# Three transfers of a fused kernel's opening are issued elsewhere: a bias on GpSimd's queue, second-layer weights behind turned blocks, and one tile's power between gathers

## The chip, the cores and the metric

The kernel runs on one core of a Trainium2 chip. Times are device microseconds of that core for one execution. The kernel before took 461.27 us in the median of three runs (460.65 to 464.81). Times in the profile are counted from the start of its span.

## The reference

The input `x` has 32 batches of 128 tokens with 512 features, all float32. Each batch has one row of conditioning `t`, and a mask that marks tokens. The reference is one block with two halves:

```
emb = silu(t) @ ada_w + ada_b;  shift, scale, gate = split(emb, 3)
norm = where(m, layernorm(x) * (1 + scale) + shift, 0)
fwd = gelu(norm @ ssm_w1 + ssm_b1) @ ssm_w2 + ssm_b2
bwd = flip(gelu(flip(norm) @ bwd_w1 + bwd_b1) @ bwd_w2 + bwd_b2)
x = x + gate * where(m, fwd + bwd, 0)
ff = silu(t) @ ffada_w + ffada_b;  shift2, scale2, gate2 = split(ff, 3)
h = gelu_tanh((layernorm(x) * (1 + scale2) + shift2) @ ff_w1 + ff_b1)
return x + gate2 * (h @ ff_w2 + ff_b2)
```

The first half counts only for the tokens that the mask marks, and these are the last tokens of each batch, at most 32 of them. The two flips cancel, since the layers work on each token alone. The second half is done for all 4096 tokens and holds most of the work.

## The kernel before

**Slots.** The marked tokens are gathered into 512 "slots", four tiles of 128. The first half is computed for slots only (`xc` holds their rows of `x`), and the new rows are written to memory in HBM, from which the second half gathers them over the rows of `x` that it has loaded. There are two such memories. `x1_wide` has the first two tiles of slots with mean and variance of each row beside it; `x1_rows` has all four tiles without them. If there are more slots, a loop at the end does the rest; in the profiled execution it does not run.

**Pairs.** The second half runs over four pairs of sides. A side is four batches, 512 tokens. Both of its matrix products are done by a Strassen-like scheme with seven products in place of eight. This needs sums of blocks of tokens (`TokenBlocks`, `token_sums`), and sums of blocks of weights: `fw1_of.combine` and `fw2_of.combine` change the weights in place, and `weight_sums(1)` to `weight_sums(4)` make further sums of the first layer's weights, which are stored to `t_rows` and loaded again for each pair (`load_weights`, into `tw`).

**Order.** The whole program is under a manual schedule: each engine works its instructions in the order in which they are written. The change lies in the opening, before the first pair's products:

- SP issues the loads of the weights and of `x`. Late among them are `raw[2]` and `raw[3]` (batches 4 to 7), the conditioning bias of the second half `modb_f` (L645, three loads of 64 KB, by `load_conditioning_bias`, L133) and its weights `ada_f` (L646, four loads of 768 KB). `modb_f` lies in the buffer of `modb_a`, the bias of the first half.
- `finish_slots(0, ...)` (L782) multiplies tile 0's result with its gate, adds `xc`, makes the statistics (`own_statistics`; its last step, the power -0.5, is on GpSimd, L178) and stores to `x1_wide` (L368) and `x1_rows` (L369).
- GpSimd gathers the new rows of batches 0 to 7 (`take_first_rows`, L792): batches 0 to 3 from tile 0 alone, 4 to 7 from tiles 0 and 1. Behind each of the first four gathers a memset on GpSimd releases one quarter of `fw2`'s load (`load_behind_gathers`, L139 and L136, 512 KB each). `finish_slots(1, ...)` stands after the third of them.
- VectorE normalises batches 0 to 3 (side 0, `normalised_of_side_0`) and transposes them in 32x32 blocks. Between the first two it makes `mod2` (`modulation_rows`, L313), the modulation of the second half, which TensorE transposes (`ptr_mod`, L850).
- TensorE goes on with the first half of slot tiles 2 and 3 (`hidden` and `project`, L207 and L224). In `hidden`, the table `after` puts other work behind each of its eight steps: `normalised_of_side_1` (batches 4 to 7), `turn_rows(0)` to `turn_rows(3)` (16 transfers of 64 KB that put side 0's blocks in place, shared by SP and ACT, L940), the stores of weight sums 1, 2 and 4, and after step 7 the two first combines of `fw2` on GpSimd and the loads for the second pair.
- `project` for tile 2 ("s2") is interleaved with TensorE's transposes of side 1 (`turn`, L929). `finish_late(2)`, `TokenBlocks.one(1)` to `one(4)` (L970) and `finish_late(3)` on VectorE follow, and TensorE starts the first pair's products (L1101), whose stream 5 is the first to read `tw`.

The transfers that SP and ACT issue share eight completion semaphores in turn: in the compiled program each of them waits for the one issued eight before it.

Of the kernel before, what the change touches and what calls it, by code (L numbers as in the profile page):

```python
# [9 lines left out]
F32 = mybir.dt.float32  # L10
# [12 lines left out]
def kernel(  # L23
# [49 lines left out]
    nc = tc.nc  # L73
    B, S, D = x.shape
    P = 128
    assert S == P
    G = 4
# [13 lines left out]
    stp = ctx.enter_context(tc.tile_pool(name="stp", bufs=4))  # L91
# [32 lines left out]
    def load_ada(t, w, blocks, width):  # L124

        for k in blocks:
            nc.sync.dma_start(t[:, k, :width], w[ts(k, P), :width])

    def load_conditioning_bias(t, vec, kinds, queue):

        rows = vec.rearrange("(m j c) -> m j c", m=3, c=P)
        for m in kinds:
            queue.dma_start(t[:, m], rows[m].unsqueeze(1).to_broadcast([KC, B, P]))  # L133

    def load_blocks(t, w):
        nc.sync.dma_start(t, w.rearrange("(k p) f -> p k f", p=P))  # L136

    def load_behind_gathers(t, w):
        nc.gpsimd.memset(t[0:1, 0, 0:1], 0.0)  # L139
        load_blocks(t, w)  # L140
# [7 lines left out]
    w2 = ssm.tile([P, HC, D], F32, name="w2")  # L148
# [20 lines left out]
    def own_statistics(t, n, name):  # L169

        for i in range(n):
            st = stp.tile([P, 6], F32, tag="st", name=f"st_{name}_{i}")
            row = t[:, i]
            nc.vector.bn_stats(st, row[:, :D])
            nc.vector.bn_aggr(row[:, D : D + 2], st)
        var = t[:, :, D + 1]
        nc.vector.tensor_scalar(var, var, EPS, None, ALU.add)
        nc.gpsimd.tensor_tensor(var, var, half[:, :n], ALU.pow)  # L178
# [22 lines left out]
    def hidden(xT, n, w, bcol, func, name, pool, parts=range(HC), after=None):  # L201

        h = []
        for f in parts:
            ph = ps_h.tile([P, 512], F32, tag="h", name=f"ph_{name}_{f}")
            for k in range(KC):
                nc.tensor.matmul(  # L207
                    ph[:, :n], w[:, k, ts(f, P)], xT[:, k, :], start=(k == 0), stop=(k == KC - 1)
                )
            t = pool.tile([P, n], F32, tag="h", name=f"h_{name}_{f}", bufs=HC)  # L210
            nc.scalar.activation(t, ph[:, :n], func, bias=biasT[:, bcol + f : bcol + f + 1])
            h.append(t)
            for g in (after or {}).get(f, ()):
                g()
        return h

    def project(i, h, w, name, between=None, bank=(ps_o, "o"), seeded=None):

        pool, tag = bank
        po = seeded or pool.tile([P, 512], F32, tag=tag, name=f"po_{name}_{i}")  # L220
        for f in range(HC):
            if between and f in between:
                between[f]()
            nc.tensor.matmul(  # L224
                po,
                h[f][:, ts(i, P)],
                w[:, f, :],
                start=(f == 0 and seeded is None),
                stop=(f == HC - 1),
                skip_group_check=seeded is not None,  # L230
            )
        return po

    def seeded_with_bias(at):
        po = ps_o.tile([P, 512], F32, tag="o", name=f"po_s{at}")
        nc.scalar.copy(po, b2)
        return po
# [111 lines left out]
    def gates_of_slots(tiles):  # L349

        strips = of_slots(
            pick, tiles, mod1, slice(2, 3), 2 * [(ps_o, "o")] + 2 * [(ps_t, "tr")], f"gate_s{tiles[0]}"
        )
        t = ssm.tile([P, len(tiles), D], F32, tag="gs", name=f"gs_{tiles[0]}")

        def to_sbuf():
            for j in range(KC):
                nc.scalar.copy(t[:, :, ts(j, P)], strips[j][:, :, 0])

        return [t[:, n] for n in range(len(tiles))], to_sbuf  # L360

    def finish_slots(at, po, gate):
        t = tp.tile([P, 1, D + 2], F32, tag="t", name=f"t_s_{at}")
        row = t[:, 0, :D]
        nc.vector.tensor_tensor(row, po, gate, ALU.mult)
        nc.vector.tensor_tensor(row, row, xc[at], ALU.add)
        own_statistics(t, 1, f"s_{at}_x1")
        nc.sync.dma_start(x1_wide[ts(at, P), :], t[:, 0])  # L368
        nc.sync.dma_start(x1_rows[ts(at, P), :], row)  # L369

    class Weights:

# [53 lines left out]
    x1_rows = dram.tile([NS, D], F32, name="x1_rows")  # L426
# [208 lines left out]
    fw2 = fwp.tile([P, HC, D], F32, name="fw2")  # L635
# [6 lines left out]
    load_raw(3)  # L642
    ada_f = adap.tile([P, KC, 3 * D], F32, tag="ada", name="ada_f")
    modb_f = adap.tile([P, 3, P], F32, tag="modb", name="modb_f", bufs=1)
    load_conditioning_bias(modb_f, ffada_b, range(3), nc.sync)  # L645
    load_ada(ada_f, ffada_w, range(KC), 3 * D)  # L646
    ph_s = {}

# [44 lines left out]
    def in_blocks(t):  # L693
        return t.rearrange("p g (h f) -> p (g h) f", f=2 * P)

    t_sum = {
        1: [in_blocks(t) for t in spare],
        2: [t_2[:, 0], t_2[:, 2]],
    }
# [17 lines left out]
    def store_weight_sums(*which, queue=nc.sync):  # L717
        for j in which:
            queue.dma_start(t_rows[j - 1, :, 4:], t_sum[j][1][:, :3])
            queue.dma_start(t_rows[j - 1, :, :4], t_sum[j][0])  # L720
# [30 lines left out]
    h1 = []  # L751
# [22 lines left out]
    gs, gates_to_sbuf = gates_of_slots(range(NC))  # L774
    po_s = [seeded_with_bias(0)]
# [3 lines left out]
    fw1_of.combine(0, 1, 2, 3)  # L779
    own_statistics(raw[2], 2, "x_2")  # L780
    b2_row = dram.tile([1, D], F32, name="b2_row")
    finish_slots(0, project(0, h1, w2, "s0", seeded=po_s[0]), gs[0])  # L782
    own_statistics(raw[3], 2, "x_3")
    t = in_blocks(group_of_tiles("tw_3"))
    t_sum[3] = [t[:, :4], t[:, 4:]]
# [4 lines left out]
    def take_first_rows(i):  # L790
        slots = P if i < G else NH
        nc.gpsimd.indirect_dma_start(  # L792
            out=raw[i // 2][:, i % 2],
            out_offset=None,
            in_=x1_wide[:slots],
            in_offset=bass.IndirectOffsetOnAxis(ap=slot_i[:, i : i + 1], axis=0),
            bounds_check=slots - 1,
            oob_is_err=False,
        )

    def take_first_rows_and_weights(i):
        take_first_rows(i)
        load_behind_gathers(fw2[:, ts(i, 2)], ff_w2[ts(i, 2 * P)])

    for i in range(3):
        take_first_rows_and_weights(i)
    finish_slots(1, project(1, h1, w2, "s1", seeded=po_s[1]), gs[1])
    take_first_rows_and_weights(3)
    for i in range(G, 2 * G):
        take_first_rows(i)  # L810

    for c in range(2):
# [43 lines left out]
    of_x = {}  # L856
# [6 lines left out]
    fw2_of = Weights(fw2, HC // 2, D // 2, t_2)  # L863
# [69 lines left out]
    def turned(xn, xT, queues, which=range(4)):  # L933

        R = 32
        src = xn.rearrange("p k i (q c) -> p q k i c", c=R)
        dst = xT.rearrange("p k (i b c) -> p b k i c", b=P // R, c=R)
        for b in which:
            for q in range(P // R):
                queues[(b + q // 2) % len(queues)].dma_start(dst[ts(q, R), b], src[ts(b, R), q])  # L940
# [406 lines left out]
    def turn_rows(b):  # L1347
        return lambda: turned(xn, xT[0], (nc.sync, nc.scalar), (b,))

    def combine_behind_weight_sums():  # L1350
        done = stp.tile([1, 1], F32, tag="done", name="done", bufs=1)
        nc.gpsimd.tensor_copy(done, t_sum[4][1][0:1, 2, 0:1])
        fw2_of.combine(0, 1, engine=nc.gpsimd)

    def load_of_pair_1():
        nc.sync.dma_start(b2_row, b2[0:1, :])
        broadcast_rows(fb2, ff_b2, nc.sync)
        x_of[1] = [load_side(1, 0, spare), None]
# [4 lines left out]
        3: [turn_rows(0), lambda: weight_sums(4)],  # L1363
        4: [turn_rows(1)],
        5: [turn_rows(2)],
        6: [turn_rows(3), lambda: store_weight_sums(1, 2, 4)],
        7: [combine_behind_weight_sums, load_of_pair_1],
    }
    h1 = hidden(xT_t, NH, w1, 0, AF.Gelu, "s1", ssm, after=after)
    nc.scalar.activation(warm, biasT[0:1, 0:1], AF.Gelu_apprx_tanh)  # L1370
# [12 lines left out]
    finish_late(2, project(0, h1, w2, "s2", {2 * k: turn(k) for k in range(KC)}, seeded=po_s[2]))  # L1383
    po = project(1, h1, w2, "s3", bank=(ps_h, "h"))
    of_x[0] = TokenBlocks(0, xT)
    for j in (1, 2, 3, 4):
        of_x[0].one(j)
    finish_late(3, po, b2)
    first_half.close()
# [285 lines left out]
```

## Time and profile before

| | us |
|---|---|
| median of the runs (lowest, highest) | 461.27 (460.65, 464.81) |
| the profiled execution | 461.85 |
| its span | 460.1 |
| busy in the span: TensorE | 448.6 |
| VectorE | 330.9 |
| ScalarE | 177.2 |
| GpSimd | 164.0 |
| mean granted TensorE clock | 0.995 |

The span is that of the profiled execution; 1.75 us of its time lie around it. An engine's busy time leaves out instructions that only issue transfers or wait. `PE` is TensorE's matmuls, `PEld` its weight loads, `DVE` VectorE, `ACT` ScalarE, `POOL` GpSimd, and `SP` the engine that mainly issues transfers; `SPq` and `ACTq` are their queues of instructions. `L368` is line 368 of the kernel. Names are the program's, with the buffer numbers left out, so `x_wide` is `x1_wide`, `fw` can be `fw1` or `fw2`, and `out<-in` says what an instruction writes and reads. A releaser (`<-DVE xn`) is what ended a wait, as the trace's semaphore events let one infer.

### The profile page before, as it was taken

What the parts mean: (1) busy time and instruction counts of PE and PEld (TensorE: products, weight loads), DVE (VectorE), ACT (ScalarE), POOL (GpSimd) and SP (SyncE); (2) the same over time, 40 slices, a digit from 0 to 9 for tenths busy, and PEclk for the clock granted to TensorE, in tenths of its full rate; (3) what the DMA queues carried; (4) which work ended last, traced back from release to release, by engine and by line L of the source; (5) the groups of instructions that cost most, each with busy time, mean ns of one, the idle gap of its engine ahead of it and who ended that gap; (6) DMA issues with size and microseconds to landing.
All of it is one profiled execution on the core that took longest, in us unless ns stands there. A gap on an engine that the chain in (4) does not pass through costs nothing.

```text
span 460.1 us, 6203 instructions
## 1 busy us (share of the span) xinstructions
PE 448.6 (97%) x2161; PEld 370.8 (81%) x2161; DVE 330.9 (72%) x568; ACT 177.2 (39%) x387; POOL 164.0 (36%) x158
## 2 busy tenths in 40 slices
PE   8999898999999999999999999999999999999995
PEld 3784485587888888888888888888888888888884
DVE  4798677879779849896786498967973996434645
ACT  3123114354355371344454614454446144552000
POOL 4210436058971000489700005887000026560000
PEclk9999989999999999999999999999999999999999
DMA  7999769772306743923087348220773342222022
GB/s 231 384 395 331 286 203 212 263 277 58 127 0 215 103 96 120 354 75 115 3 228 105 80 150 333 97 84 11 220 110 74 127 171 81 80 89 95 0 86 102
DMA packets 83405, 70.98 MB, mean 154 GB/s; under 512 B 63160, under 2 KB 64520, under 8 KB 82346
## 3 DMA queue, kind: packets, MB, share of 16 engines
q1 hardware_dynamic: 68438, 58.60, 40.9%
q0 software_dynamic: 4160, 10.54, 6.7%
q10 hardware_dynamic: 10772, 1.39, 2.2%
q8 instruction: 19, 0.31, 0.3%
q14 instruction: 16, 0.13, 0.1%
HBM read 56.84 MB, written 13.70 MB: 153 GB/s over the span
## 4 chain that ended last, share of the span: by engine, by line
PE 85%; DMA 6%; POOL 4%; issue 3%; DVE 2%; POOLq 0%; SPq 0%; DVEq 0%
PE a_o L1288 23%; PE a_m L1101 18%; PE e_o L1288 18%; PE e_m L1101 14%; PE po_s L224 5%; DMA x_wide<-t_s 3%; POOL x L869 2%; PE ph_s L656 2%; PE ph_s L207 2%; DMA xc<-in_x_dram,token_i_s 1%; POOL x L792 1%; DMA tw<-t_rows 1%; DMA x<-x_wide,slot_i 1%; PE last L1288 1%; PE pm_keep_clock L446 1%
## 5 line engine op out<-in xcount | busy, mean ns | idle before, releaser
L1152 POOL TENSOR_TENSOR ha<-p_m,ha 128x512 f32<-128x512 f32 x20 | 25.8, 1288 | 166.9 <-ACT ha L1159 142.1
L1288 PE MATMUL e_o<-fw,ha 128*128 128x256 f32 x256 | 57.9, 379 | 0.0
L923 ACT ACTIVATE xT<-xT,modT 128x128 f32<-128x128 f32 x112 | 44.2, 480 | 32.2 <-DMA xT<-xn 32.2
L1288 PE MATMUL a_o<-t,hb 128*128 128x256 f32 x240 | 54.1, 379 | 0.0
L1288 PEld LDWEIGHTS e_o<-fw,ha 128*128 128x128 f32 x256 | 48.6, 190 | 6.6
L1288 PEld LDWEIGHTS a_o<-t,hb 128*128 128x128 f32 x240 | 45.6, 190 | 6.2
L1063 ACT ACTIVATE hb<-hb,biasT 128x256 f32<-128x256 f32 x64 | 29.0, 500 | 29.7 <-POOL hb L1185 19.3
L1115 ACT COPY p_m<-e_m 128x512 f32<-128x512 f32 x27 | 15.8, 586 | 47.0 <-PE e_m L1101 39.6
L869 POOL DMA_INDIRECT x<-x_rows,slot_i x24 | 28.6, 1192 | 6.3 <-issue 5.4
L1152 POOL TENSOR_TENSOR hb<-p_m,hb 128x512 f32<-128x512 f32 x20 | 29.4, 1470 | 0.3
L1288 PE MATMUL a_o<-fw,ha 128*128 128x256 f32 x128 | 29.0, 379 | 0.0
L1288 PE MATMUL a_o<-t,s 128*128 128x256 f32 x128 | 28.9, 379 | 0.0
L1288 PE MATMUL e_o<-fw,s 128*128 128x256 f32 x128 | 28.9, 379 | 0.0
L224 PE MATMUL po_s<-w,h_s 128*128 128x512 f32 x64 | 28.4, 594 | 0.0
L1159 ACT COPY ha<-e_m 128x512 f32<-128x512 f32 x32 | 18.5, 579 | 25.1 <-PE e_m L1101 23.4
L1126 DVE TENSOR_TENSOR e_m<-a_m,ha 128x512 f32<-128x512 f32 x20 | 13.9, 697 | 18.4 <-POOL ha L1152 7.4
L1288 PEld LDWEIGHTS a_o<-fw,ha 128*128 128x128 f32 x128 | 24.2, 190 | 3.4 <-ACT a_o L1227 0.2
L1288 PEld LDWEIGHTS e_o<-fw,s 128*128 128x128 f32 x128 | 24.3, 190 | 3.3
L1288 PEld LDWEIGHTS a_o<-t,s 128*128 128x128 f32 x128 | 24.3, 190 | 3.3
L1063 ACT ACTIVATE ha<-e_m,biasT 128x256 f32<-128x256 f32 x48 | 20.1, 469 | 15.4 <-PE e_m L1101 11.4
L1101 PE MATMUL a_m<-xT,tw 128*128 128x256 f32 x96 | 24.6, 379 | 0.0
L1101 PE MATMUL e_m<-s,fw 128*128 128x256 f32 x92 | 23.8, 381 | 0.0
(237 smaller groups left out, 898.5 us busy)
## 6 DMA issues: line engine op xcount, KB each, us to landing
tw<-t_rows SPq DMA_DIRECT2D x16, 896.0 KB
x<-in_x_dram SPq DMA_DIRECT2D x16, 512.0 KB
gate<-gate_rows POOLq DMA_DIRECT2D x8, 1024.0 KB
out_dram<-x SPq DMA_DIRECT2D x15, 512.0 KB
xT<-xn SPq DMA_DIRECT2D x92, 64.0 KB
ada_f<-in_L_cond_ffada_w_dram SPq DMA_DIRECT2D x4, 768.0 KB
ada_a<-in_L_cond_ada_w_dram SPq DMA_DIRECT2D x4, 512.0 KB
w<-in_L_cond_ssm_w_dram SPq DMA_DIRECT2D x2, 1024.0 KB
```

Of the source, the lines that this page charges most:

```text
L207: nc.tensor.matmul(ph[:, :n], w[:, k, ts(f, P)], xT[:, k, :], start=(k == 0), stop=(k == KC - 1))
L224: nc.tensor.matmul(po, h[f][:, ts(i, P)], w[:, f, :], start=(f == 0 and seeded is None), stop=(f == HC - 1), skip_group_check=seeded is no ...
L656: nc.tensor.matmul(ph_s[f][:, ts(c, P)], w1[:, k, ts(f, P)], xT_s[:, k, ts(c, P)], start=(c == 0 and k == 0 and f % 2 == 0), stop=(k == KC ...
L869: nc.gpsimd.indirect_dma_start(out=xs[i // G][i % G // 2][:, i % 2], out_offset=None, in_=x1_rows, in_offset=bass.IndirectOffsetOnAxis(ap= ...
L923: nc.scalar.activation(out, src, AF.Identity, bias=shift, scale=scale)
L1063: nc.scalar.activation(dst[:, n], src[:, n], AF.Gelu_apprx_tanh, bias=biasT[:, f : f + 1])
L1101: nc.tensor.matmul(bank[:, ts(n, QT)], self.w_block(j, product)[:, ts(n, P)], self.x_block(j, product), start=(product in ("P1", "P5") and ...
L1115: nc.scalar.copy(p5, e)
L1126: nc.vector.tensor_tensor(e, a, p5, add)
L1152: nc.gpsimd.tensor_tensor(self.place(RESULT[j], c), self.p5[j], other, ALU.add)
L1159: nc.scalar.copy(self.place(RESULT[j], c), src)
L1288: nc.tensor.matmul(part, src[:, k, ts(i, P)], w[product][:, k, :], start=(last and k == 0), stop=True, skip_group_check=True,)
```

## The change

1. The three loads of `modb_f` are issued by GpSimd, behind the two gathers of slot tiles 2 and 3, and no longer by SP ahead of `ada_f`.
2. `fw2` is loaded by one transfer of 2 MB in place of four, and it is issued behind step 6 of `hidden`, after the last of the turned blocks, with one memset.
3. `finish_slots` stores to `x1_wide` only and returns a function for the store to `x1_rows`; both such stores are issued after the weight sums' stores.
4. `finish_slots(1, ...)`, and so the power of the second tile on GpSimd, stands after two of the gathers of `take_first_rows`, not after three.
5. The stores of weight sums go in the order 4, 1, 2.
6. The first two combines of `fw2` are done by VectorE, between the second and the third block sum of tokens, no longer by GpSimd.

```diff
-        nc.sync.dma_start(x1_rows[ts(at, P), :], row)
+        return lambda: nc.sync.dma_start(x1_rows[ts(at, P), :], row)
...
-    load_conditioning_bias(modb_f, ffada_b, range(3), nc.sync)
+    load_conditioning_bias(modb_f, ffada_b, range(3), nc.gpsimd)
...
-    finish_slots(0, project(0, h1, w2, "s0", seeded=po_s[0]), gs[0])
+    store_rows = [finish_slots(0, project(0, h1, w2, "s0", seeded=po_s[0]), gs[0])]
...
-    def take_first_rows_and_weights(i):
+    for i in range(2):
         take_first_rows(i)
-        load_behind_gathers(fw2[:, ts(i, 2)], ff_w2[ts(i, 2 * P)])
-
-    for i in range(3):
-        take_first_rows_and_weights(i)
-    finish_slots(1, project(1, h1, w2, "s1", seeded=po_s[1]), gs[1])
-    take_first_rows_and_weights(3)
-    for i in range(G, 2 * G):
+    store_rows.append(finish_slots(1, project(1, h1, w2, "s1", seeded=po_s[1]), gs[1]))
+    for i in range(2, 2 * G):
         take_first_rows(i)
...
-    def combine_behind_weight_sums():
-        done = stp.tile([1, 1], F32, tag="done", name="done", bufs=1)
-        nc.gpsimd.tensor_copy(done, t_sum[4][1][0:1, 2, 0:1])
-        fw2_of.combine(0, 1, engine=nc.gpsimd)
-
...
-        6: [turn_rows(3), lambda: store_weight_sums(1, 2, 4)],
-        7: [combine_behind_weight_sums, load_of_pair_1],
+        6: [turn_rows(3), lambda: load_behind_gathers(fw2, ff_w2), lambda: store_weight_sums(4, 1, 2)] + store_rows,
+        7: [load_of_pair_1],
...
-    for j in (1, 2, 3, 4):
+    for j in (1, 2):
+        of_x[0].one(j)
+    fw2_of.combine(0, 1)
+    for j in (3, 4):
         of_x[0].one(j)
```

## The prediction

> **What bounds the kernel now.** The share of busy time on the page says that TensorE is the bound: 448.6 of 460.1 us. Only the other 11.5 us, and time in which TensorE runs slowly, can be won. So I read first what TensorE waited for (engine, line, releaser, us, times, longest):
>
> ```profile
> PE ptr_mod L850 <- DVE mod L313: 2.4, 1, 2.4
> PE ptr L929 <- DVE xn L825: 1.9, 2, 1.1
> ```
>
> Both lie between 55 and 75 us, and both are VectorE being late. The table of stages agrees: TensorE busy 7.62 of 10 us in 50-60 and 13.09 of 15 in 60-75, then full until 105. The last 4.6 us of the span are no concern of this change. Next, the chain that ended last, in that stretch:
>
> ```profile
> 46.43 6.26 DMA x_wide<-t_s
> ...
> 58.09 6.83 DMA x_wide<-t_s
> ...
> 70.39 3.57 DMA x<-x_wide,slot_i
> ...
> 73.98 0.56 DVE xn L825
> ...
> 74.58 0.33 PE ptr L929
> 74.91 1.72 PE po_s L224 x4
> ```
>
> VectorE is late because the rows it normalises come by a store to `x1_wide` (6.3 and 6.8 us) and a gather back, and GpSimd waits out both stores. Such a store need not take that long: `tw<-t_rows`, 896 KB on an idle queue at 92.69, landed in 4.25 us; at the 395 GB/s of a full queue its bytes are 2.3 us, so some 1.9 us are fixed, and 257 KB should take 0.7 + 1.9 = 2.6 us. What stood ahead is seen in SP's own queue (start, us, instruction):
>
> ```profile
> 29.86 7.68 SPq L133 DMA_DIRECT2D modb_f<-in_L_cond_ffada_b_dram  x3
> 37.63 3.72 SPq L127 DMA_DIRECT2D ada_f<-in_L_cond_ffada_w_dram  x4
> ...
> 54.70 3.22 SPq L136 DMA_DIRECT2D fw<-in_L_cond_ff_w_dram  x3
> 58.09 0.34 SPq L368 DMA_DIRECT2D x_wide<-t_s  x1
> ```
>
> Ahead of the first store lie 3 MB of `ada_f`, held back 7.7 us by three 64 KB loads; ahead of the second, three 512 KB pieces of `fw2`. The table in half microseconds (stretch, length, TensorE clock, DMA share, GB/s) shows what the small loads cost: at 389 GB/s before, the queue falls to a mean of 246 over 38.5-43.5, which is 5 x (1 - 246/389) = 1.8 us lost.
>
> ```profile
> 38.00:38.50 0.50, 1.00 1.05 389
> 38.50:39.00 0.50, 1.00 0.52 189
> ...
> 42.50:43.00 0.50, 1.00 0.93 171
> 43.00:43.50 0.50, 1.00 0.54 190
> ```
>
> Last, the same table for TensorE (length, busy, clock, DMA share, GB/s): soon after the 2.4 us stop its clock is 0.50 from about 59.2 to 62.6.
>
> ```profile
> 58.50:59.00 0.50, 0.50 (x4) 1.00 1.10 356
> 59.50:60.00 0.50, 0.50 (x3) 0.50 0.62 152
> 62.00:62.50 0.50, 0.50 (x2) 0.50 0.86 324
> 63.00:63.50 0.50, 0.50 (x4) 1.00 1.04 398
> ```
>
> [...] one stretch of 3.4 us at 0.50. In the window before it (55.7-59.1) TensorE stood 2.1 of 3.4 us, 60%; in 72.8-76.2 it stood 1.6 us, 47%, and the clock stayed. [...] The DMA share of 1.02 to 1.06 in 16-38 us agrees: there is no spare bandwidth where the bias goes. [...]
>
> **Part by part.**
>
> *The bias, 3 x 128 packets of 512 B, SP to GpSimd.* `modb_f` takes `modb_a`'s buffer, whose last reader ends at 22.4 + 0.3 = 22.7. GpSimd then issues three (nearest row: `gate_rows`, 4 in 2.17 us; a gather takes 1.0 to 1.2), so 2 to 3.6 us, done by 26.3; its next work is the root at 26.14, needed only at 30.9. Issue cost: nothing. For the DMA engines the nearest case is the 64 KB of `modb_a` on ACT's queue, in the table of queues for 10-12 us (packets, MB, share of 16 engines):
>
> ```profile
> q10 hardware_dynamic: 147, 0.07, 13.8%
> ```
>
> 13.8% of 16 engines for 2 us is 0.28 us a load, 0.83 for three, against 1.8 + 0.5 (their bytes) = 2.3 us where they are now. So the opening's queue drains 1.5 us earlier at its end (bounds: 0.3, only the gap at 38.5-40; 2.3, nothing left), but everything behind 22.7 us comes 0.8 later at first. `fw1` lands at 36.7 instead of 35.9, so the four combines and the statistics behind it end at 43.6, and tile 0's finish starts 0.45 us later. `w2`'s second half lands at about 39.4, just before TensorE needs it (39.5).
>
> *First store.* Issued at 46.9, landed at about 51.0 (52.7 - 1.5, and the `x1_rows` store no longer beside it). Gather 0 starts 0.8 later and its rows are there 2.5 after that, as now: 54.3. VectorE's first block also writes over `tw_3`, whose store is issued at 50.1-50.9: 2.3 + 1.9 gives about 54.8. That one decides: VectorE starts at 54.8 instead of 56.0, and the stop of 2.4 us becomes 1.2.
>
> *Clock.* [...] 3.4 us at half speed, 1.7 us, come back.
>
> *Second tile's power, and `fw2` out of the way.* The power runs after gather 1 instead of gather 2, without memsets: its store goes out at 54.9 instead of 58.1, with nothing of `fw2` ahead, and lands at 57.5 instead of 64.9. The last four gathers then start at 58.2 and, at 1.5 us each, the last at 62.8, rows by 66.4 at the 3.6 us seen now (73.95 before). VectorE reaches side 1 at 64.9 and is done at 67.0, before TensorE asks at 68.9. The stretch 71.85 to 74.91, 3.06 us for transposes that take 0.44, loses its 2.6 us of stops and of single transposes.
>
> Sum to the start of `project` "s2": 1.2 + 1.7 + 2.6 = 5.5 us (74.9 becomes 69.4).
>
> *The combines, GpSimd to VectorE.* Two at 1.23 us between the second and third block sums, 2.46 us. GpSimd's 4.7 us were beside other work, so removing them wins nothing. What hides the new ones is VectorE's idle time:
>
> ```profile
> 90.00 0.69 DVE L1377 TENSOR_TENSOR t_s<-po_s,b 128x512 f32<-128x512 f32 x1 [0.73 <-PE po_s L224]
> ...
> 94.39 0.70 DVE L1126 TENSOR_TENSOR e_m<-a_m_alone,p_m 128x512 f32<-128x512 f32 x1 [1.04 <-PE a_m_alone L1101]
> ```
>
> 0.73 + 1.04 = 1.77 is covered and about 0.6 (less some overlap of neighbours) is not. Behind the wait stand the two block sums, `finish_late(3)` and the sum that (1,P3) on TensorE needs: 0.6 us lost. They also wait for `fw2`, below.
>
> *`fw2` and the stores behind the turned blocks.* SP's eight turned issues (8.65 us) start when side 0 is transposed, at 62.5, and end at 71.1; then come `fw2` 2 MB, 2.7 MB of sums, and the rest up to the load of `tw` for stream 5: 7.2 MB; before, `fw2` and two row stores were not among them (4.6 MB). At 395 GB/s from 72.4 (the last turned blocks share the engines) `fw2` lands at 79.7; VectorE asks for it at 87.0 - 5.5 = 81.5, so 1.8 us to spare. The queue is through at 90.6, `tw` adds 2.3 + 1.9 and lands at 94.8; TensorE needs it at 99.3 - 5.5 + 0.6 = 94.4. Loss 0.4 us (bounds: 0, and 2.7 if the slow stretch at 84-88, 2.3 us under full rate in the trace, comes again). Moving the `x1_rows` stores back costs nothing: the gathers that read them start at 100.1 - 4.5. The order 4, 1, 2 matters only for the buffer of the fourth sums, free at about 83.
>
> Forecast: 5.5 - 0.6 - 0.4 = 4.5 us. The profiled execution took 461.85 us (460.1 and 1.75 around it): 457.35. The median shown is 0.6 lower and the runs spread by more, perhaps with and without the slow clock, so I say 457.2.
>
> **The rivals.** *All of it hides* (`tw` in time, combines half covered, queue drained 2.3 earlier): 5.7 to 6.3 us, 455.2 to 456.2. For it: the full 6.0 us (4.3 of stops, 1.7 of clock) is really lost. Against: VectorE is nearly full from 84 to 94. *A late `tw`* replaces the stops: 2 to 3 us at (5,P5), 458.3 to 460.3; for it, the margin above is already negative. *The first stop and the slow clock stay*, because the queue's end hardly moves: only 2.6 less 1.0 is won, 460.2; against it, 1.8 us of lost rate are plain. *Slower*: `fw2` mixes with the turned blocks. These move 139 GB/s at a DMA share near 1 (70-77 us). Should 2.1 MB go at that pace, it needs 15 instead of 5.3 us and lands at 89.4; VectorE stands 8 us at the combine, `tw` comes near 104.5, TensorE stands 10 us: 461.85 - 4.9 + 10.1 = 467. It decides against the change from a `tw` 4.9 us late. Against it: the blocks are nearly drained when `fw2` is issued.
>
> **How the numbers follow.** About 1% (4.6 us) is what a measurement of this kernel can tell from no change. Chances: forecast (456.2 to 458.3) 0.50, all hides 0.17, late `tw` 0.20, first stop stays 0.07, slower 0.06. Under 456.7, faster by over 1%, lie all of the second and a third of the first: 0.33. Slower by over 1%: 0.06. Within: 0.61. The range from 455.2 to 460.3 takes the first three, less their tails: 0.83.
>
> **What the changed profile would show.** Right: `x_wide` stores at about 4 and 2.6 us; no wait of `ptr` on `xn`; `ptr_mod` waiting 1.2; clock 1.0 throughout 55-65; no dip at 38.5-43.5; `fw2` landed before VectorE's combines; (1,P3) waiting some 0.6. Wrong would make it: VectorE idle ahead of the combines, TensorE idle ahead of the first `tw` product, a clock that still halves, or `w2` coming too late for `project` "s0" because the bias went first.

## The result and the profile after

The changed kernel takes 458.43 us in the median of 16 runs (457.43 to 461.48), beside 463.89 us for the kernel before in 16 runs on the same chip (460.56 to 465.76). The ratio is 0.9901, with a 95% interval of 0.9876 to 0.9925. The profiled execution took 457.94 us with a span of 456.2 us, where the kernel before had 461.85 and 460.1. The span is 3.9 us shorter and the median 5.5: the kernel before varies more, and the execution that its page shows lies at the fast end of its runs. In the comparisons of this document disturbed executions are left out; that concerns one experiment, where three of six took some 10 us longer. Each experiment has its own runs of the kernel before beside it, so that median differs a little from one to the next.

TensorE's busy time went from 448.6 to 445.3 us, VectorE's from 330.9 to 332.8, GpSimd's from 164.0 to 161.2. First what TensorE waited for in the changed kernel (engine, line, releaser, us, times, longest); line numbers past L800 are 5 lower than before, past L1350 7 to 10.

```profile
PE e_m L1096 <- DMA tw<-t_rows: 2.3, 1, 2.3
...
PE po_s L224 <- DMA w<-in_L_cond_bwd_w_dram: 0.9, 1, 0.9
PE e_m L1096 <- DVE e_m L1121: 0.6, 1, 0.6
PE ptr_mod L845 <- DVE mod L313: 0.4, 1, 0.4
```

The 2.4 us at `ptr_mod` are 0.4 now, and the 1.9 us of transposes that waited for side 1 are gone. Three waits took their place: for `tw`, for VectorE at (1,P3), and for the second half of `w2`, which no longer comes in time. Next the chain that ended last (start, us, what).

```profile
47.42 3.63 DMA x_wide<-t_s
...
51.84 2.95 DMA x<-x_wide,slot_i
...
56.60 0.44 PE ptr_mod L845 x2
...
70.44 11.23 DMA fw<-in_L_cond_ff_w_dram
...
89.10 8.09 DMA tw<-t_rows
...
97.33 1.10 PE e_m L1096 x4
```

Before, both stores to `x1_wide` stood in this chain, with 6.3 and 6.8 us; now the first takes 3.6 and the second is not in it. `fw2` and `tw` are. SP's own queue of instructions (start, us, instruction) shows the weights and the second store:

```profile
31.26 4.44 SPq L127 DMA_DIRECT2D ada_f<-in_L_cond_ffada_w_dram  x4
...
55.42 0.32 SPq L368 DMA_DIRECT2D x_wide<-t_s  x1
```

The second store goes out at 55.4 with nothing of `fw2` ahead of it; the gathers that need it start at 59.25. TensorE's clock in that stretch (stretch, length, busy, clock, DMA share, GB/s) is 1.00, where the half microseconds from 59.5 to 62.5 showed 0.50 before:

```profile
54.00:66.00 12.00, 11.61 (x57) 1.00 0.33 63
66.00:75.00 9.00, 9.00 (x38) 1.00 0.94 177
```

Where the time went is best read by laying the same product of both traces side by side. These are starts on TensorE, read from its timeline in each kernel (L1101 before, L1096 after):

| product | before | after | earlier by |
|---|---|---|---|
| first of the pair, `a_m_alone<-xT,fw` | 89.80 | 84.45 | 5.35 |
| first behind (1,P3), `a_m_alone<-xT,t` | 96.11 | 91.41 | 4.70 |
| first with `tw`, `e_m<-sx,tw` | 99.56 | 97.33 | 2.23 |
| `e_m<-xT,fw`, behind GpSimd's sums | 116.70 | 112.94 | 3.76 |
| `a_m<-xT,tw` near 140 | 140.11 | 136.25 | 3.86 |

So 5.35 us were won ahead of the products, 0.65 went at (1,P3), 2.47 at `tw`, and then 1.53 came back. From the first `tw` product to `e_m<-xT,fw` the kernel before took 17.14 us and the changed one 15.61. The last of these products, first before, then after:

```profile
116.70 1.13 PE L1101 MATMUL e_m<-xT,fw 128*128 128x256 f32 x4 [0.44 <-DVE e_m L1145]
```

```profile
112.94 1.03 PE L1096 MATMUL e_m<-xT,fw 128*128 128x256 f32 x4
```

The kernel before loses the 1.53 in two places. 0.66 goes in short gaps up to the product that starts at 112.38 (109.49 in the changed kernel); VectorE, which makes the sums for these products, has no listed stop there. The other 0.87 goes between that product and the one at 116.70, which waits for VectorE's sum L1145, and that for GpSimd, whose chain of eight gathers and three sums runs from 100.08 to 115.91. In the changed kernel the same chain runs from 95.88 to 111.67 and TensorE, held back by `tw`, does not meet it. Two runs below in which `tw` is in time and the gathers are spread take 16.26 us for the same stretch: they win the 0.87 and not the 0.66. So GpSimd's part is shown by a run, VectorE's is read from its timeline alone. Part of what the `tw` wait took had been lost before at these places.

### The profile page after: what moved, and what is told of

Same layout as the page of the kernel before. It is cut to its first block, busy times and chain, and to the rows that moved or that the text cites. A ratio compares the mean times of both kernels' runs of the same rounds, so it can differ in the third digit from the quotient of the medians.

```text
span 456.2 us, 6196 instructions
## 1 busy us (share of the span) xinstructions
PE 445.3 (98%) x2161; PEld 370.9 (81%) x2161; DVE 332.8 (73%) x570; ACT 176.9 (39%) x387; POOL 161.2 (35%) x155
## 4 chain that ended last, share of the span: by engine, by line
PE 80%; DMA 13%; DVE 4%; SPq 1%; issue 1%; POOL 0%; ACT 0%; POOLq 0%; ACTq 0%; DVEq 0%
PE a_o L1283 23%; PE a_m L1096 20%; PE e_o L1283 18%; PE e_m L1096 15%; DMA fw<-in_L_cond_ff_w_dram 7%; DMA tw<-t_rows 2%; DMA w<-in_L_cond_ssm_w_dram 1%; PE ph_s L207 1%; DVE t L387 1%; DMA xT<-xn 1%; DMA x_wide<-t_s 1%; PE last L1283 1%; SPq L935 1%; DMA x<-x_wide,slot_i 1%; DVE fw L387 0%
## 5 line engine op out<-in xcount | busy, mean ns | idle before, releaser
L1096 PE MATMUL a_m<-xT,tw 128*128 128x256 f32 x96 | 24.7, 380 | 0.0
L1126 DVE TENSOR_TENSOR hb<-a_m,hb 128x512 f32<-128x512 f32 x20 | 13.7, 685 | 15.0 <-PE a_m L1096 15.0
```

The source lines that it names most:

```text
L1096: nc.tensor.matmul(bank[:, ts(n, QT)], self.w_block(j, product)[:, ts(n, P)], self.x_block(j, product), start=(product in ("P1", "P5") and ...
L1126: nc.vector.tensor_tensor(dst, a, dst if prior else self.p5[j], add)
```

## The experiments

**The bias alone** (the kernel before with the first edit):

```diff
-    load_conditioning_bias(modb_f, ffada_b, range(3), nc.sync)
+    load_conditioning_bias(modb_f, ffada_b, range(3), nc.gpsimd)
```

> The kernel before with part 1 alone: the three bias loads on GpSimd's queue. Theory (the bias only hands time from the queue's end to its front): w2's second half comes late and TensorE waits 0.9 us in project s0; the first x_wide store lands near 51; the stop at ptr_mod falls from 2.4 to about 0.5 and the clock stays at 1.0; but the second store still lies behind fw2's pieces, so the stop ahead of side 1's transposes grows to about 3 us. Span 458.5 (460.1 before). Rival (each microsecond won at the first stop reaches the end): 2.0 of stop and 1.7 of clock less 0.9, span 457.3. Second rival (the packets only move): 460.

Measured: 462.33 us (460.19 to 464.38, 20 runs; before 463.87), ratio 0.9968 (0.995 to 0.9987), span 460.3 against 460.1. TensorE's waits:

```profile
PE ptr L929 <- DVE xn L825: 2.7, 3, 1.2
...
PE po_s L224 <- DMA w<-in_L_cond_bwd_w_dram: 0.8, 1, 0.8
PE ptr_mod L850 <- DVE mod L313: 0.6, 1, 0.6
```

The first stop fell from 2.4 to 0.6, but 0.8 of it had only moved to `w2`, and side 1's stop grew from 1.9 to 2.7. The slow clock moved with it: the clock is 1.00 from 55 to 65 us, but 0.50 from 74.4 to 77.8, behind side 1's stop. In the 3.4 us ahead of that TensorE stood for 1.7. So `project` "s2" starts 1.2 us earlier than before (73.54), and the first product of the pair 0.5 later (90.28). The theory had seen the growing stop and not the clock. The span agrees with the second rival (460), but it is a weak witness: the page of the kernel before lies 2.0 us under its median, this one 0.3. At the median the first edit alone gives 1.5 us.

**TensorE kept busy** (the kernel before, with nine 128x128 products of the identity ahead of the transposes of `ptr_mod`, whose results nothing reads):

```diff
+        idle = ps_t.tile([P, 512], F32, tag="tr", name="idle")
+        for _ in range(9):
+            nc.tensor.matmul(idle[:, :P], ident, ident, start=True, stop=True)
```

> The kernel before with nine 128x128 multiplications of the identity ahead of ptr_mod, which fill about 2 us of the first stop with work that nobody reads. Theory (a stop halves the clock, and the rows of side 1 set the start of its transposes): the clock stays at 1.0 between 55 and 65 us, hidden ends 1.7 us earlier, and the stop ahead of side 1's transposes grows by as much; span unchanged, 460.0. Rival (the clock's 1.7 us reach the end by themselves): 458.4. Second rival (the stop is not what halves the clock): 0.5 still appears.

Measured: 463.9 us (20 runs; before 463.87), ratio 1.0009 (0.9991 to 1.0028), span 460.0. The table of stretches of this kernel shows the clock back at 1.00, and its waits that side 1's stop grew from 1.9 to 2.5:

```profile
58.00:62.00 4.00, 4.00 (x20) 1.00 0.88 251
```

```profile
PE ptr L932 <- DVE xn L825: 2.5, 3, 1.3
```

In the kernel before, the same stretch had a clock of 0.65. So the slow clock was real and by itself cost next to nothing: side 1's rows hardly came earlier (`project` "s2" starts at 74.34, 0.4 us earlier than before). Only with them earlier can the 1.7 us of the clock count.

**The power alone** (the kernel before, with `finish_slots(1)` after two gathers, `fw2` left with the gathers):

```diff
-    for i in range(3):
+    for i in range(2):
         take_first_rows_and_weights(i)
     finish_slots(1, project(1, h1, w2, "s1", seeded=po_s[1]), gs[1])
-    take_first_rows_and_weights(3)
+    for i in range(2, 4):
+        take_first_rows_and_weights(i)
```

> The kernel before, with the second tile's power after two gathers instead of three and nothing else: the four loads of fw2 stay with the gathers, two ahead of its store instead of three. Theory (the second store waits for what stands ahead of it in the queue): it is issued near 55 instead of 58.1 and lands near 60.5 instead of 64.9; the last gather and side 1's rows follow some 3 to 4 us earlier, the 1.9 us of transposes waiting for xn go, the first stop at ptr_mod (2.4) and the slow clock stay; project s2 starts 2.5 us earlier and the span is 457.5. Rival (the third and fourth piece of fw2 now stand beside the store and the last gathers): the store lands near 63, half of the stop stays, span 459.

Measured: 460.68 us (459.55 to 462.18, 10 runs; before 463.16), ratio 0.9947 (0.9924 to 0.997), span 458.2. The waits:

```profile
PE ptr_mod L851 <- DVE mod L313: 2.4, 1, 2.4
...
PE e_m L1102 <- DVE e_m L1146: 0.4, 1, 0.4
```

The first stop stays, side 1's is gone, and the first product starts at 87.68, which is 2.12 us earlier than before. The same difference stands at every later product: here nothing is lost to `tw`, since `fw2` is loaded early. This one move gives about half of what the whole change gives. The waits are those of the theory; the span lies halfway between its 457.5 and the rival's 459.

**The bias back on SP's queue** (the changed kernel without its first edit):

```diff
-    load_conditioning_bias(modb_f, ffada_b, range(3), nc.gpsimd)
+    load_conditioning_bias(modb_f, ffada_b, range(3), nc.sync)
```

> The changed kernel without part 1: the bias loads back on SP. Theory (the load of tw for stream 5 sets the end now, so what is lost at the first stop is found again there): no wait for w2, stop at ptr_mod about 2, perhaps the slow clock, and the wait for tw shrinks from 2.3 to between 0.5 and 2; span 456.2 to 457.2 (456.2 for the changed kernel). Rival (the bias is what made the gain): the stop of 2 and the clock's 1.7 come back in full, less 0.9: span 459.

Measured: three runs of 457.25, 457.96 and 458.27 us, spans 455.5 to 456.6, ratio to before 0.9886 (0.9847 to 0.9924). Within the changed kernel the first edit makes no difference that these runs can show, and the rival's span of 459 is not met. There is no profile of these three, so where the first stop went in them is not shown.

**No bias at all** (the changed kernel with the three loads replaced):

```diff
-    load_conditioning_bias(modb_f, ffada_b, range(3), nc.gpsimd)
+    nc.gpsimd.memset(modb_f, 0.0)
```

> The changed kernel with the three loads of the conditioning bias left out (a memset of zeros stands in their place; the bias is zeros in these inputs), so that 384 packets of 512 bytes are gone from the opening's queue. It gives their price there. Prediction's price: 0.83 us, so fw1 lands 0.8 us earlier than in the changed kernel. Rival price, from the dip at 27.5 to 31 us in the changed kernel's table: 1.75 us, so the second half of w2 comes in time, the 0.9 us wait of po_s goes and fw1 lands 1.5 to 1.8 us earlier. To the end: theory (tw's landing sets it): what is won in the opening is lost at stream 5, whose wait for tw grows, span 455.9 to 456.3. Rival (tw's load moves with all that stands ahead of it): the whole 0.9 to 1.3 us come through, span 455.

Measured: 456.07 us (455.99 to 457.36, 4 runs; before 463.16), ratio 0.9851 (0.9824 to 0.9878), span 454.3. The price in the opening is plain. The table of half microseconds, first of the changed kernel, then of this one:

```profile
27.50:28.00 0.50, 0.50 (x4) 1.00 1.08 251
...
29.00:29.50 0.50, 0.50 (x4) 1.00 1.01 223
```

```profile
27.50:28.00 0.50, 0.50 (x4) 1.00 0.98 373
...
29.00:29.50 0.50, 0.50 (x4) 1.00 0.99 393
```

The DMA share is 1 in both; with the bias in it the queue moves 57% and 67% of the bytes. VectorE's first combine of `fw1`, which starts when `fw1` has landed, answers in its timeline, again changed kernel first:

```profile
37.41 1.23 DVE L387 TENSOR_TENSOR t<-fw 128x1024 f32<-128x1024 f32 x1 [3.12 <-DMA fw<-in_L_cond_ff_w_dram]
```

```profile
35.81 1.22 DVE L387 TENSOR_TENSOR t<-fw 128x1024 f32<-128x1024 f32 x1 [0.48 <-DMA fw<-in_L_cond_ff_w_dram]
```

The 384 packets cost 1.6 us there: the rival price, not the prediction's 0.83. The other traces of this document say the same: this combine starts between 37.2 and 38.1 in the six that have the bias on GpSimd's queue, and between 35.7 and 36.3 in the others. But at the first product this is worth only 0.36 us (84.09 against 84.45). The larger part of the 1.9 us in the span, 1.34, is won at `tw`: TensorE waits 1.0 us for it and not 2.3. The reason is in the queue's rate. Changed kernel, then this one:

```profile
88.50:89.00 0.50, 0.50 (x5) 1.00 1.66 135
...
89.50:90.00 0.50, 0.30 (x2) 1.00 0.62 98
```

```profile
88.50:89.00 0.50, 0.50 (x4) 1.00 1.01 360
...
89.50:90.00 0.50, 0.00 (x0) 1.00 1.09 385
```

From 87 to 91 the changed kernel's queue moved a mean of 217 GB/s, this one 338; against the 400 around it that is 1.8 and 0.6 us lost. Why the slow stretch is shorter here, these runs do not show. It need not be the missing bias, 60 us earlier: the run with the combines on GpSimd, below, has the bias and moves 359 GB/s from 87 to 91. Neither theory is confirmed: the gain came through, but not by the way that the rival gave.

**`fw2` behind `tw`** (the changed kernel; the load of `fw2` after both loads of `tw`, its first two combines in VectorE's later streams):

```diff
-        6: [turn_rows(3), lambda: load_behind_gathers(fw2, ff_w2), ...
+        6: [turn_rows(3), ...
...
-    fw2_of.combine(0, 1)
...
     now.load_weights(2)
+    load_blocks(fw2, ff_w2)
...
+            put(5, 3, fw2_of.combine, 0)
+            put(6, 4, fw2_of.combine, 1)
```

> The changed kernel with fw2's 2 MB issued behind the first two tw loads, and its two combines in VectorE's windows of streams 3 and 7. Theory (fw2 ahead of it is why tw is late): tw lands 4 to 5 us earlier, TensorE waits neither for it (2.3 us) nor at (1,P3) (0.6 us); span 453.3. Rival (the queue's slow stretch at 87 to 90 us makes tw late whatever is ahead of it): 1 to 2 us of the wait stay, span 454.5 to 455.5. Second rival (the combines stall the windows they are put into, or fw2 is late for the second product): a new wait after 110 us, span 456 or more.

Measured: 458.43 us (457.67 to 458.58, 4 runs), ratio 0.9893 (0.9863 to 0.9923), span 456.0. Both waits are gone, and the first `tw` product starts at 94.19, 3.14 us earlier than in the changed kernel. At 137 us 0.12 of these 3.14 are left. Its waits name three of the places:

```profile
PE a_o L1283 <- ACT a_o L1222: 0.5, 1, 0.5
PE e_m L1096 <- DVE e_m L1121: 0.5, 1, 0.5
PE e_m L1096 <- DVE e_m L1140: 0.4, 1, 0.4
```

The last is at 111.32, behind GpSimd's gathers, the other two at 122.41 and 136.99, behind the combines. From the first `tw` product to 111.32 this kernel takes 17.13 us, as the kernel before did: the 1.5 us that came back in the changed kernel are lost again, partly in gaps that no row lists, with products of 0.86 us coming every 0.9 to 1.2. The other 1.5 go near the two combines. These are what the second rival had named, and the span is the one it gave (456 or more); GpSimd's chain nobody had named.

**The combines on GpSimd** (the changed kernel, the two combines of `fw2` moved only):

```diff
-        7: [load_of_pair_1],
+        7: [lambda: fw2_of.combine(0, 1, engine=nc.gpsimd), load_of_pair_1],
...
-    fw2_of.combine(0, 1)
```

> The changed kernel with its two fw2 combines on GpSimd instead of VectorE, nothing else. Theory (tw sets the end here, not VectorE): the 0.6 us at (1,P3) goes, and the wait for tw grows from 2.3 to 2.9 us by just that; stream 5 begins at 97.3 as before and the span stays 456.2. Rival (the combines also delay what leads to tw's load, or to the sums behind it): stream 5 begins 0.6 us earlier or more, span 455.6 or less. A third way: GpSimd's combines (4.7 us together, in the kernel before) hold up its gathers, which end at 108 us, and a wait on GpSimd at 111 us appears: span 457 to 460.

Measured: 460.94 us (459.04 to 461.44, 6 runs), ratio 0.9953 (0.9928 to 0.9979), span 457.3. None of the three ways: the wait at (1,P3) grew. The waits, and VectorE's timeline:

```profile
PE e_m L1096 <- DVE e_m L1121: 2.4, 1, 2.4
...
PE e_m L1096 <- DMA tw<-t_rows: 0.9, 1, 0.9
```

```profile
80.94 1.22 DVE L965 TENSOR_TENSOR s<-s,xT 128x1024 f32<-128x1024 f32 x1
82.09 3.37 DVE L965 TENSOR_TENSOR xT<-xT,xT 128x1024 f32<-128x1024 f32 x1
85.38 3.37 DVE L965 TENSOR_TENSOR s<-xT,s 128x1024 f32<-128x1024 f32 x1
```

GpSimd's combines run at 81.54 (2.83 us) and 84.45 (3.22 us). Two of VectorE's sums, of the same form as the one before them, take 3.37 us each beside them and not 1.22: 4.3 us lost to save 2.46. They end at 85.46 and 88.75, each 1.1 us after the GpSimd instruction beside it (84.37 and 87.67). That 1.1 us is nearly the 1.22 us that such a sum takes alone, so by these times they did not run slowly: each seems to have stood until that one was over. This is inferred from the times, and what held the sums up is not shown. In the kernel before, the same two combines (76.85 to 81.63) stood beside VectorE's scalings from PSUM, twelve in 4.11 us from 76.52, and slowed nothing: that is 0.34 us each, and without GpSimd four took 1.36 us in the changed kernel (69.93).

**`fw2` in the idle gap** (the changed kernel; `fw2` issued behind the fourth gather, its combines on GpSimd, and the first pair's gathers spread over the streams as those of later pairs are):

```diff
     for i in range(2, 2 * G):
         take_first_rows(i)
+        if i == 3:
+            load_behind_gathers(fw2, ff_w2)
...
-        7: [load_of_pair_1],
+        7: [lambda: fw2_of.combine(0, 1, engine=nc.gpsimd), load_of_pair_1],
...
-    take_first_half(1, x_of[1])
+    take_first_half(1, x_of[1], range(G))
```

> Three edits on the changed kernel: fw2 is loaded behind the fourth gather, where the queue stands idle (53.5 to 62.5 us in the changed kernel's trace), its two combines run on GpSimd behind the fourth weight sums, and the first pair's gathers are spread over its streams as those of later pairs are. Theory (three ends follow each other closely: tw's landing, 2.3 us at 97.3; VectorE's combines, 0.6 us at 90.4; GpSimd's chain of gathers, 0.45 us at 111.3): with all three moved away, the 3.1 us that the run with fw2 behind tw had at 94.2 and then lost stay to the end: no wait of e_m on tw, none at 111.3, span 453.1 (456.2 less 3.1), time about 454.9. Rival 1 (fw2 in the gap runs into gathers 4 to 7): side 1's rows come up to 5.3 us later (2.1 MB at 395 GB/s), transposes of side 1 wait for xn again by 1 to 3 us, span 454 to 456. Rival 2 (the spread gathers come too late for their readers in pair 1, or GpSimd's combines hold them up): a new wait of VectorE on GpSimd past 111, span 455.5 to 457.

Measured: 460.08 us (459.6 to 460.89, 4 runs), ratio 0.9925 (0.99 to 0.995), span 459.2. Rival 1, and dearer than it said. The first `tw` product is not waited for any more, but the first product of the pair comes 5.23 us later than in the changed kernel:

```profile
PE ptr L926 <- DVE xn L822: 2.7, 1, 2.7
PE ptr L926 <- DVE xT L918: 1.3, 1, 1.3
```

```profile
70.28 2.60 DVE L822 TENSOR_SCALAR xn<-x 128x512 f32<-128x512 f32 x1 [0.79 <-DMA x<-x_wide,slot_i]
```

The last row of side 1 reaches VectorE at 70.28 and not 67.39, and there the instruction of 0.55 us takes 2.60. GpSimd's combine started just before it, at 70.26, and ran 2.34 us; that this held it up is inferred from the times. The queue was idle in that gap, but the rows in it were awaited.

**`fw2` ahead of the last turned blocks** (the changed kernel, one step earlier in `after`):

```diff
-        5: [turn_rows(2)],
-        6: [turn_rows(3), lambda: load_behind_gathers(fw2, ff_w2), ...
+        5: [turn_rows(2), lambda: load_behind_gathers(fw2, ff_w2)],
+        6: [turn_rows(3), ...
```

> The changed kernel with the load of fw2 issued on SP two of its eight turned transfers earlier, so that two megabytes stand beside the turned blocks of the last tile. It measures the price of the slower rival, in which fw2 mixes with turned blocks. Rival of the prediction (they go at the blocks' pace, 139 GB/s): fw2 lands at 85 to 89 us, VectorE stands 3 to 8 us at the combines, tw lands 5 or more us later than its 97.2, span 461 to 466. Theory ([...]the blocks are nearly drained): fw2 lands within 1 us of 81.7, the last turned blocks 1 to 4 us later, TensorE's first product (84.45) at most 1.5 us later, span 456.2 to 457.7.

Measured: 461.56 us (460.05 to 462.96, 9 runs; before 463.9), ratio 0.9955 (0.9928 to 0.9981), span 458.3. The span is just above the theory's 457.7 and below the rival's 461 to 466; the first product of the pair is not late (84.27). The place of the loss is the rival's, the mechanism is not. `fw2` is early: SP's queue waits for its landing until 79.3. ScalarE's first scaling of the turned blocks starts at 80.03 in place of 74.43, and VectorE's second block sum waits for it; TensorE stands 3.4 us at (1,P3):

```profile
80.03 6.30 ACT L918 ACTIVATE xT<-xT,modT 128x128 f32<-128x128 f32 x16 [8.18 <-DMA t_rows<-tw]
```

```profile
83.27 1.22 DVE L965 TENSOR_TENSOR s<-s,xT 128x1024 f32<-128x1024 f32 x1 [3.11 <-ACT xT L918]
```

The releaser named in the first line is a store of weight sums, with which the blocks share completion semaphores. Whether the blocks or that store ended the wait is not told apart. After the stop TensorE's clock fell to 0.50 from 94.5 to 97.5. Against the changed kernel this costs 2.1 us of span and 3.1 at the median.

**The bias behind the first store** (the changed kernel; the three loads on SP's queue right after the first `x1_wide` store, and the addition of 1.0 moved down to the sum that reads it):

```diff
-    load_conditioning_bias(modb_f, ffada_b, range(3), nc.gpsimd)
...
     store_rows = [finish_slots(0, project(0, h1, w2, "s0", seeded=po_s[0]), gs[0])]
+    load_conditioning_bias(modb_f, ffada_b, range(3), nc.sync)
```

> The changed kernel with the three bias loads out of the full part of the opening's queue: issued on SP's queue right behind the first x_wide store (47.4 us in the changed kernel's trace, where the queue runs dry), with the addition of 1.0 to the scale rows moved down to the sum that reads them. Theory (the 384 packets cost some 1.7 us where the queue is full and next to nothing where it isn't; what they cost came through to the end): the opening as in the run without bias loads (fw1 35.8, project s2 69.0, wait for tw 1.0), span 454.3 to 454.8, time 456.1 to 456.6. Rival (the packets beside the store and the first gathers hold those up as they did the weights): the store or gather 0 comes 0.8 to 1.7 us later, VectorE starts side 0 at 55.5 or later, the stop at ptr_mod is 1 to 2 us, span 455.3 to 456.3.

Measured: 457.3 us (457.04 to 461.3, 6 runs), ratio 0.9888 (0.9847 to 0.993), span 455.3. The opening is relieved (`fw1` at 36.06, no wait for `w2`), but gather 0 starts at 52.25 and not 51.84, released by the bias:

```profile
52.25 1.09 POOL L791 DMA_INDIRECT x<-x_wide,slot_i  x1 [2.70 <-DMA modb_f<-in_L_cond_ffada_b_dram]
```

The stop at `ptr_mod` is 1.0 us and the first product comes 0.67 later than in the changed kernel. The 0.9 us of the span came at `tw` once more, which starts its products 0.81 earlier, with the slow stretch of its queue short again (mean 281 GB/s over 88 to 90, 360 to 393 in the half microseconds after it). So on the opening the stop and the span are at the lower end of what the rival gave, and the end is not explained by the bias.

**Loads for the next pair behind `tw`** (the run before, with the `x` loads of side 0 moved behind the first `tw` load, the bias row of the second layer behind all of them), and the same **with the gathers spread**:

```diff
-        broadcast_rows(fb2, ff_b2, nc.sync)
-        x_of[1] = [load_side(1, 0, spare), None]
...
     now.load_weights(1)
-    x_of[1][1] = load_side(1, 1)
+    x_of[1] = [load_side(1, 0, spare), None]
     now.load_weights(2)
+    x_of[1][1] = load_side(1, 1)
+    broadcast_rows(fb2, ff_b2, nc.sync)
```

```diff
-    take_first_half(1, x_of[1])
+    take_first_half(1, x_of[1], range(G))
...
-            if p:
-                put(2, 6, take_first_half, p + 1, x_next, range(G, G + 2))
+            put(2, 6, take_first_half, p + 1, x_next, range(G, G + 2))
```

> The run before it (bias behind the first store), with the two x loads of the next pair's side 0 and the broadcast of the ff bias row moved from ahead of the first tw load to behind it. Theory (tw is late because of the bytes and the slow row ahead of it): its load has 1 MB, 2.7 us, less ahead; the wait for tw of 1.0 goes, stream 5 starts 1.0 us earlier and that stays: span 453.3 to 453.8. Rival (GpSimd's gathers, which need those x loads first, end as late as before and are now the limit near 111 us): a wait on VectorE's e_m behind GpSimd's sums of up to 1.0 us, span 454.3 to 454.8.

> The run before it, with the first pair's eight gathers spread as later pairs have them (four at once, the others in streams 2, 3 and 5). If GpSimd's chain of gathers is the next limit, its sums come 6 us earlier, the wait near 111 us is gone and the span is 453.3 or less. If it is not, the span is that of the run before within 0.3 us; if the late gathers delay the sums of the second half, a new wait on GpSimd between 112 and 135 us makes it 0.5 to 1.5 us longer.

Measured: 458.5 us (457.19 to 460.23, 6 runs), ratio 0.9892 (0.9855 to 0.993), span 457.4 for the first; 457.09 us (456.43 to 458.99, 6 runs), ratio 0.9875 (0.9838 to 0.9912), span 454.9 for the second. In both the first `tw` product starts 1.8 to 1.9 us earlier than in the changed kernel, with no wait for `tw`. In the first GpSimd gives it back. Its chain and TensorE's waits:

```profile
92.67 9.74 DMA x<-in_x_dram
...
113.49 0.71 DVE e_m L1140
...
114.24 1.13 PE e_m L1096 x4
```

```profile
PE e_m L1096 <- DVE e_m L1121: 2.1, 2, 1.6
...
PE e_m L1096 <- DVE e_m L1140: 0.4, 1, 0.4
```

The gathers write over rows of `x` that land at 102.4, 9.7 us after the last step of their issue, and the sums behind the gathers are late, by 2.0 us where the rival had up to 1.0; the span misses the theory's (453.3 to 453.8) and the rival's (454.3 to 454.8). With the gathers spread the waits on GpSimd are gone and 1.2 us stay to the end, but the span is 454.9 and not the 453.3 of the expectation. In these two the queue moves 399 and 408 GB/s from 84 to 88 us, without the slow stretch that the kernel before has there (166) and the changed one from 87 to 91 (217). What was moved, the 1 MB of `x` or the bias row, seems to belong to that stretch. These runs do not part the two, and a shorter slow stretch (143 to 260 GB/s from 90.5 to 92 in the second run) stands at the `tw` loads. This last version is 1.3 us below the changed kernel in span and at the median, but the two intervals of the ratios overlap, so it is not shown to be faster.

## Why the prediction was right, point by point

The time, 458.43, lies in the range (455.2 to 460.3) and 1.2 above the forecast of 457.2. That puts it at the edge between the forecast's own band (to 458.3) and that of the rival "a late `tw`" (from 458.3), and the rival tells better what happened: TensorE waits 2.3 us for `tw`, where it said 2 to 3. Two of the four signs that were to show the prediction wrong are there, this wait and the late `w2`.

The gain in the profile is 3.9 us where the sum said 4.5. Two errors behind this nearly cancel, and that is luck: `tw` cost 1.9 us more than was put down for it, and 1.5 us came back that stood in no sum. At the median the gain is 5.5; the forecast set out from 461.27, the median of three runs, which 16 runs put at 463.89. What the longer executions of the kernel before wait for, no trace shows.

- *Queue's end and the first store.* "Landed at about 51.0", "VectorE starts at 54.8": measured 51.05 and 54.81. What decided is not as forecast, though: the trace names the rows of the gather, which landed at 54.79 (forecast 54.3), and not the store of weight sums. The price of a 257 KB store, 2.6 us, was an estimate from one `tw` load: the two took 3.6 and 3.1 us. The packets' price was mis-sized: 0.83 us, taken from `modb_a` on ScalarE's queue in 10 to 12 us, against 1.6 us measured by leaving them out. The share of the engines in that row, 13.8% over 2 us, did not hold where the queue is full. `fw1` came at 37.4, not 36.7, and `w2`'s second half came too late for TensorE (0.9 us here; 0 to 0.5 in the traces of the four experiments that share this opening with the changed kernel). The stop at `ptr_mod` is 0.4 and not 1.2, because TensorE arrives that much later: 0.9 + 0.4 is the same loss in two places.
- *Clock.* As forecast, 1.00 (54 to 66 us). That a stop of 1.2 us would leave it there was the author's estimate from two stretches of one trace. With side 1's rows early it counts: the 56 products behind `ptr_mod` take 12.25 us, and 13.94 in the run with the power alone, which keeps the slow clock. That it is worth anything only together with side 1 is what the identity products showed. How much standing halves the clock is not shown. In the kernel before, from 72.8 to 76.2, TensorE's busy time is 1.95 of 3.4 us, so it stood for 43%, not 47%; in the run with the bias alone 50% in 3.4 us were followed by a clock of 0.50; and the stop of 2.3 us at `tw`, which is 68% of the 3.4 us up to 97.4, left the clock at 1.00. The length of a stop alone does not decide.
- *Side 1.* As forecast: no stop, and `project` "s2" starts 5.35 us earlier (forecast 5.5). The power alone gives 2.1 us of it.
- *Combines.* 0.6 us at (1,P3), measured 0.6. The run with them on GpSimd shows that VectorE was the better place at this time, for a reason that the prediction did not have: two sums of 3.37 us in place of 1.22.
- *`fw2` and `tw`.* Here the sum failed: `fw2` "lands at 79.7", measured 81.67. VectorE is free for it at 81.65 and takes it at 81.69: no wait, but the 1.8 us to spare are used up. `tw` "lands at 94.8", measured 97.2, and the loss is 2.3 and not 0.4. It stayed inside its bounds (0 to 2.7): the slow stretch of the kernel before, set aside as a bound, came again at 87 to 91 and cost 1.8 us by its rate. Its cause is open; the runs with late loads narrow it. The rows of `fw2` and `tw` also came through a queue that from 70 to 75 us, with turned blocks in it, moved 120 to 301 GB/s, where the prediction counted full rate from 72.4. From 72.4 to 75 that is a mean of 271 for 395, some 0.8 us. The two together, less the little that the queue gained elsewhere, are the 2.4 us by which `tw` is late.
- *Not in the sum at all:* 1.5 us that the kernel before lost between 99.6 and 116.7 and the changed one does not. The prediction's table of stages had TensorE full until 105 and it looked no further. The runs with `tw` early show that GpSimd's chain of gathers stands right behind, for 0.9 of it.
- *Not run alone:* the later stores to `x1_rows`, the order 4, 1, 2 and the one transfer of 2 MB for four. What each of them is worth is not shown.

## What to carry to other kernels

Lay two traces side by side, product by product: a gain of 5.35 us that ends as 3.9 had been lost and found at three places, and the table of waits shows only some of them. When one late transfer is removed, ask what stands next behind it: here TensorE met in turn `tw`, VectorE's combines and GpSimd's gathers, each within 1 to 3 us, and taking away one alone was worth nothing. Price small packets on a full queue by what the queue loses (1.6 us here), not by the time that they take on an emptier one (0.83), and do not fill a queue's gap that lies in front of rows that are awaited: here the first product of the pair came 5.23 us later.

## What the runs showed of the hardware that was not expected

- Beside GpSimd's combines of `fw2`, VectorE's sums of 1024 elements took 3.37 us and not 1.22, each ending 1.1 us after GpSimd's (the combines on GpSimd), and a normalisation of 512 elements 2.60 and not 0.55 (`fw2` in the idle gap); twelve scalings from PSUM took 4.11 us beside such combines, no more for each than four in 1.36 us without.
- 384 packets of 512 bytes on GpSimd's queue cost 1.6 us of a full queue, for 0.5 us of bytes: where they run, it moved 251 and 223 GB/s, and 373 and 393 without them.
- With 2 MB issued just ahead of the last four turned transfers of 64 KB, ScalarE started on the turned blocks 5.6 us later (80.03 and not 74.43), while the 2 MB themselves were there when wanted (79.3).
- TensorE's clock fell to 0.50 for 3.4 us behind a stretch of 3.4 us in which it had stood for 50% in three short stops (the bias alone), and stayed at 1.00 behind one stop of 2.3 us (the changed kernel).
- A stretch of the queue near 87 to 91 us runs at about half its rate for 1 to 4 us, and its length differs between kernels that issue the same transfers there: a mean of 217 GB/s over these 4 us in the changed kernel and of 359 with the combines on GpSimd, beside 372 in the 2 us behind it in the changed one.
